# A message-passing layer on one core: three VectorE operations made in two halves each

## The chip, the cores and the metric

One Trainium2 chip, one of its cores. The metric is device microseconds of one execution of the whole program. In the profile PE is TensorE (matmul), PEld its weight load, DVE is VectorE, ACT is ScalarE, POOL is GpSimd and SP the engine that issues most DMAs; "L750" is line 750 of the kernel.

## The reference

One layer of a graph network with a residual: 6250 nodes of 128 features, 200000 edges sorted by `dst`, 20 edge features. With `ssp(x) = softplus(x) - log 2`:

```python
h = maximum(layernorm(x), 0)
xw = h @ W_in                                             # 6250 x 128
W_ij = (ssp(f_ij @ W_f1 + b_f1) @ W_f2 + b_f2) * cutoff   # 200000 x 128
x_ij = xw[dst] * W_ij                                     # idx_j = dst, gathered
out = segment_sum(x_ij, src, 6250)                        # idx_i = src, scattered
return x + ssp(out @ W_o1 + b_o1) @ W_o2 + b_o2
```

Everything is float32; the kernel gets there with sums of bfloat16 parts.

## The kernel before, in words

The edges are cut into chunks of 128; four chunks are a quad, so that 391 quads pass through one loop over `i`, a software pipeline in which iteration `i` works on different steps of several quads. The order inside an iteration is written out by hand: fixed steps and, between them, named points ("D0", "DM", "DR", "D2", "L" and so on) at which further steps are run. The table `AT` gives each step its offset in iterations and its point; the order on each engine is therefore the order of the program.

A quad's path: TensorE makes the filter's first layer `z` (L375), ScalarE its softplus by exponential and logarithm (L380, L385); TensorE gathers the rows of the nodes `xg` with a one-hot matrix (L563) and makes the second layer `W` (L571); ScalarE scales the gathered rows by the cutoff into `xc` (L576, four a quad); VectorE multiplies both (`s2_m`, L586). The message is then summed into the nodes in one of two ways, and the quads alternate between them.

- Scattered quads (184 by lists, 13 plain). The message tile is called `s` (or `m`). GpSimd adds its rows to one of four accumulators in DRAM by indirect DMAs (L648), 128 rows each, four per quad. A row index comes from a list: within a window of 16 such quads each lane finds which of its edges have the same node. The equality rows for it are made on VectorE by `l_eq` (L431, 92 times, one per two quads: four blocks of 128 x 2 columns, the nodes of a quad pair against each lane's own node), counted on TensorE and used for the index tile `lji`. Duplicates of a lane go through a list of their own in the accumulator, which is read back (`lm`, L517), summed by equal node on TensorE (`lsum`, L535), copied to `os` (L541) and scattered once more with the index `oji` (L838).
- Permuted quads (194). The message tile is called `pt`, four chunks of 388 columns: 128 for the message, 128 for its first remainder, 128 for its second and four more. A float32 message is split into three bfloat16 parts: a part is the upper half of the float32 word, and `part_rem` (L750, twice a quad, point "DM" and point "DR" of the same iteration) subtracts it from what is left. TensorE permutes the parts into groups of nodes with a one-hot matrix `pm` (VectorE, L736; TensorE, L762 and L785), ScalarE copies them to `sg` (L770), a DMA regroups them as `mst` (L777), and once in eight quads TensorE sums a round of them into units (`un`, L867) with one-hot matrices `so` (VectorE, L849), which VectorE adds to `accT` (L883).

The edge features are split into three bfloat16 parts in the same way, one block of 4096 edges at a time (49 blocks of 128 x 640 columns): `fb_1` and `fb_3` copy on ScalarE, `fb_2` makes the first remainder (L329), `fb_4` the second (L337), which a DMA writes to DRAM with the other two parts.

After the loop the accumulators are added, transposed and sent through the last two layers (lines from 1530 on).

```python
if first <= i - 1 < NQ:
    s2_m(i - 1)          # between the points "DM" and "DR"
```

Of the kernel before, what the change touches and what calls it, by code (L numbers as in the profile page):

```python
# [13 lines left out]
ALU = mybir.AluOpType  # L14
# [6 lines left out]
P = 128  # L21
# [55 lines left out]
def tile_gnn(ctx: ExitStack, tc: tile.TileContext, x, fB, cT, srcT, srcr, srci, dstr, win_, wf1, wf2, bias, bo1c, wo1,  # L77
             wo2, consts, ident, cmap, out, n_edges):
    nc = tc.nc
# [6 lines left out]
    FE = RB * BE // P  # L86
# [71 lines left out]
    fst = {}  # L158
# [8 lines left out]
    srcT_sb = cp.tile([P, EP // P], I16, name="srcT_sb")  # L167
# [166 lines left out]

    def fb_4(b):
        f3 = fst[b]["f3"]
        nc.vector.tensor_tensor(f3[:, 2], fst[b]["fr"], f3[:, 1], op=ALU.subtract)  # L337
        nc.sync.dma_start(fsd[b].rearrange("g (p e) -> p g e", p=P), f3)
        late["fb"] = fst.pop(b)["f"]

# [55 lines left out]
    sbs = {}  # L396
# [31 lines left out]
    def l_eq(k):  # L428
        n = 2 * k
        eq = wk.tile([P, 4, P, 2], BF16, tag="eql", name="eql", bufs=2)  # L430
        nc.vector.tensor_tensor(eq, sbs.pop(k).rearrange("p (b i t) -> p b i t", b=4, t=2),  # L431
                                srcT_sb[:, n * 4:n * 4 + 8].rearrange("p (b t) -> p b t", t=2).unsqueeze(2)
                                .to_broadcast([P, 4, P, 2]), op=ALU.is_equal)
        lst["eq", k] = eq

    def l_count(g):
# [303 lines left out]
    def high(t):  # L740
        return t.bitcast(BF16)[:, :, 1::2]
# [4 lines left out]

    def part_rem(q, k):
        pt = mp[q]["pt"]
        a = pt[:, :, (k - 1) * P:k * P]
        nc.vector.tensor_tensor(pt[:, :, k * P:(k + 1) * P], a, high(a), op=ALU.subtract)  # L750
        if k == 2:
            del st[q]

# [177 lines left out]
    with tc.manual_schedule():  # L931
# [72 lines left out]
        fb_3(0)  # L1004
        fb0 = fst[0]["f"]
        fb_4(0)
        rel0 = rel(0, 0, SC, "pt", pool=pg)
        prep_x1(0)
# [54 lines left out]
        def put(name, base, fn, *a, busy=()):  # L1063
            d, point = AT[name]
            i = max(clear(base + d, busy) if busy else base + d, 0)
            at(i, point, fn, *a)
            return i
# [51 lines left out]
        for b in range(1, NB):  # L1119
            t0 = 2  # L1120
            if b > 1:
                t0 = 8 * b - 8
                while t0 + 1 not in mpi or t0 + 1 in units:
                    t0 -= 1
                at(max(6, t0 - 6), "L", fb_load, b)
            if b > 1:
                at(max(8, t0 + AT["fmax"][0]), AT["fmax"][1], fb_max, b)
            else:
                at(7, "D2", fb_max, b)
            put("f1", t0, fb_1, b)  # L1130
            put("f2", t0, fb_2, b)
            put("f3", t0, fb_3, b)
            put("f4", t0, fb_4, b)
# [87 lines left out]
        if spread:  # L1221
            k = clear(mid + 9, busy, 2)
# [3 lines left out]
            k = clear(NQ - 1, busy, 2)  # L1226
# [19 lines left out]
        for g in range(len(tgroups)):  # L1246
            i = clear(max(r0_at + 1, ret_at + 12), units)
# [4 lines left out]
        for r in range(1 if min(2, NQ) and spread else 0, -(-len(mpq) // RKQ)):  # L1252
            i = mpq[RKQ * r]
            early = i < 8
            i = max(i, 4)
            put("rk_group", i, rank_group, r)
            put("rk_local", i, rank_local, r)
            k = put("rk_count", i, rank_count, r, busy=units)
            k = max(k + 1, i + AT["rk_own"][0])
            at(k, AT["rk_own"][1], rank_own, r)  # L1260
            k = clear(max(k, i + AT["rk_over"][0]), units)
            at(k, AT["rk_over"][1], rank_over, r)
            k = max(k + 1, i + AT["rk_slot"][0])
# [5 lines left out]
        for w in range(NW):  # L1269
            for g in range(wsize[w] // 4):  # L1270
                n = LB + SW * (w - 1) + 4 * g - LSHIFT
                i = splain[n] + 2 if w else 7 + 3 * g
                while w and (i not in mpi or i in units):
                    i -= 1
                for k in range(2):
                    kk = (LB + SW * w + 4 * g) // 2 + k
                    at(max(0, i + k - 2), "L", sb_load, kk)
                    put("l_eq", i + k, l_eq, kk)
                i = put("l_count", i, l_count, (LB + SW * w) // 4 + g, busy=units)
                k = put("l_dup", i, l_dup, w, g)  # L1280
            i = put("l_scan", i, l_scan, w)
            i = put("l_before", i - 1, l_before, w, busy=units)
# [3 lines left out]
            i = put("l_place", i, l_place, w, busy=units)  # L1286
            put("l_take", i, l_take, w)
            i = clear(max(wend[w] + wlag[w], uslots[-1][-1] + 1 if w == NW - 1 else 0), units)
# [4 lines left out]
            k = clear(i + AT["l_sum"][0], units)  # L1293
# [4 lines left out]
            k = put("l_int", k, over_int, ("L", w))  # L1298
# [4 lines left out]
        for q in mpq:  # L1303
            put("pm", q, perm_oh, q)
            put("rem1", q, part_rem, q, 1)
            put("rem2", q, part_rem, q, 2)
            put("ext", q, part_ext, q)
            if q + 4 in units:
# [12 lines left out]
            if mpi[q] % 2 or q == mpq[-1]:  # L1321
                k = mpq[mpi[q] + 1] if mpi[q] + 1 < len(mpq) else q + 3
# [4 lines left out]
                k = put("over_row", q, over_row, q, busy=units)  # L1327
                put("over_eq", k, over_eq, q)
                k = put("over_sum", q, over_sum, q, busy=units)
                put("over_copy", k, over_copy, q)  # L1330
                put("over_ji", k, over_ji, q)
                k = put("over_int", k, over_int, q)
# [122 lines left out]
    with tc.For_i(0, redo, 1):  # L1455
# [8 lines left out]
        with tc.For_i(0, trips, 1) as ci:  # L1464
# [15 lines left out]
            sb = wk.tile([P, P], I32, bufs=1, tag="oeq", name="fsb")  # L1480
# [27 lines left out]
            a = wk.tile([P, P], F32, tag="a", name="fa")  # L1508
# [7 lines left out]
            eq = wk.tile([P, P], F32, tag="eq", name="feq", bufs=3)  # L1516
# [15 lines left out]
    pt = ctx.enter_context(tc.tile_pool(name="pt", bufs=2, space=PSUM))  # L1532
# [150 lines left out]
def clear(i, busy, n=1):  # L1683
    while any(i + k in busy for k in range(n)):
        i += 1
    return i
# [114 lines left out]
```

## Time and profile before

| | |
|---|---|
| Three runs | 1875.44, 1885.99, 1892.93 us (median 1885.99) |
| The profiled execution | 1863.7 us |
| Its span, first to last instruction | 1861.9 us |
| TensorE matmul busy | 1663.2 us (89%) |
| VectorE busy | 1612.2 us (87%), 4740 instructions |
| ScalarE busy | 1466.1 us (79%) |
| GpSimd busy | 1486.0 us (80%), 949 instructions |
| Mean granted clock of TensorE | 0.971 of full speed |
| DMA | 339.68 MB, mean 182 GB/s |

Busy time counts overlapping instructions of an engine once. Instructions of one engine run in the order of the program. A row that names a line with "x4" groups four instructions that follow each other; "idle before" is the time in which the engine did nothing ahead of a group, and the arrow names what ended it. "issue" means that the profile shows nothing that the engine waited for. The shapes are partitions x elements. A timeline gives the start from the beginning of the span.

### The profile page before, as it was taken

How to read it: one execution, taken by the hardware profiler on the slowest of the kernel's cores; microseconds unless marked ns; L12 is line 12 of the kernel's file. 1: busy time of each engine (PE TensorE's matmuls, PEld its weight loads, DVE VectorE, ACT ScalarE, POOL GpSimd, SP SyncE). 2: the span in 40 equal slices, each digit the busy share in tenths (PEclk: the TensorE clock that was granted, in tenths of full speed). 3: DMA queues.
4: the chain of work that ended last, by engine and by line, in shares of the span. 5: the costliest groups of instructions: out<-in, count | busy, mean ns of one | idle time of the engine just before them, and what ended most of it. 6: DMA issues, size and time to landing. Idle time of an engine off the chain costs nothing.

```text
span 1861.9 us, 55503 instructions
## 1 busy us (share of the span) xinstructions
PE 1663.2 (89%) x19308; PEld 1114.3 (60%) x19308; DVE 1612.2 (87%) x4740; ACT 1466.1 (79%) x4068; POOL 1486.0 (80%) x949
## 2 busy tenths in 40 slices
PE   4779988999999989999898999999999999999846
PEld 3556656666666656656665666666666666666624
DVE  5778989899899989898899799899888899888746
ACT  4778878888888888888787888888888888888505
POOL 4567778888888888888888888888887888887875
PEclk9889999999999999999999999999999999999978
DMA  8998888888888888888887898888888888888847
GB/s 289 249 215 201 209 172 164 187 177 180 180 180 163 186 165 178 180 176 167 171 188 158 175 192 164 183 187 174 182 174 169 185 175 172 175 163 175 189 67 265
DMA packets 365471, 339.68 MB, mean 182 GB/s; under 512 B 86686, under 2 KB 328781, under 8 KB 365187
## 3 DMA queue, kind: packets, MB, share of 16 engines
q1 hardware_dynamic: 234005, 270.57, 49.7%
q0 software_dynamic: 130624, 65.33, 33.9%
q8 instruction: 152, 2.49, 0.5%
q14 instruction: 132, 1.08, 0.2%
q10 hardware_dynamic: 558, 0.20, 0.0%
HBM read 150.76 MB, written 108.08 MB: 139 GB/s over the span
## 4 chain that ended last, share of the span: by engine, by line
PE 36%; DVE 28%; DMA 12%; ACT 11%; issue 6%; SPq 4%; POOL 3%; DVEq 0%; ACTq 0%; POOLq 0%
PE un L867 10%; PE W L571 8%; PE pq L762 6%; DMA mst<-sg 5%; PE po L785 5%; DVE pt L750 4%; DVE accT L883 4%; ACT sg L770 4%; PE z L375 3%; DVE pm L736 3%; POOL acc L648 3%; ACT xc L576 3%; DVE s L586 2%; DMA acc<-s,lji 2%; DMA ft<-fsd 2%
## 5 line engine op out<-in xcount | busy, mean ns | idle before, releaser
L648 POOL DMA_INDIRECT acc<-s,lji x736 | 1182.1, 1606 | 244.1 <-issue 175.8
L576 ACT ACTIVATE xc<-xg,cb 128x128 f32<-128x128 f32 x1564 | 444.3, 370 | 7.1 <-PE xg L563 6.7
L571 PEld LDWEIGHTS W<-w,a 128*128 128x128 f32 x3128 | 426.5, 198 | 37.5 <-issue 23.7
L867 PE MATMUL un<-so,mst 32*128 32x392 bf16 x9312 | 431.6, 327 | 7.0 <-ACT sg L770 2.7
L571 PE MATMUL W<-w,a 128*128 128x128 f32 x3128 | 425.7, 280 | 0.1
L770 ACT CAST sg<-pq 128x388 bf16<-128x388 f32 x776 | 345.1, 493 | 78.5 <-DMA mst<-sg 38.1
L762 PE MATMUL pq<-pt,pm 128*128 128x388 bf16 x1552 | 328.3, 335 | 29.5 <-ACT mo L790 9.6
L867 PEld LDWEIGHTS <-mst 32*128 32x128 bf16 x9312 | 231.3, 93 | 155.5 <-issue 11.8
L385 ACT ACTIVATE a<-a,con 128x512 f32<-128x512 f32 x391 | 282.4, 722 | 11.6
L750 DVE TENSOR_TENSOR pt<-pt 128x512 f32<-128x512 f32 x388 | 263.6, 679 | 0.0
L380 ACT ACTIVATE a<-z 128x512 f32<-128x512 f32 x391 | 241.0, 616 | 25.7 <-PE z L375 25.5
L762 PEld LDWEIGHTS <-pm 128*128 128x128 bf16 x1552 | 146.3, 97 | 138.7 <-issue 46.0
L849 DVE TENSOR_SCALAR so<-iot,mst 128x392 bf16<-128x392 f16 x776 | 217.8, 330 | 5.3 <-PE un L867 4.7
L883 DVE TENSOR_TENSOR accT<-un,accT 128x392 f32<-128x392 f32 x368 | 182.0, 555 | 45.1 <-PE un L867 43.1
L736 DVE TENSOR_SCALAR pm<-iotp,pos 128x384 bf16<-128x384 f16 x776 | 208.9, 329 | 0.0
L648 POOL DMA_INDIRECT acc<-os,oji x109 | 175.0, 1606 | 37.4 <-issue 15.2
L375 PE MATMUL z<-ft,ws 123*128 123x512 bf16 x391 | 153.9, 394 | 41.9 <-ACT a L380 14.8
L586 DVE TENSOR_TENSOR s<-W,xc 128x512 f32<-128x512 f32 x184 | 125.7, 683 | 68.6 <-ACT xc L576 58.3
L586 DVE TENSOR_TENSOR pt<-W,xc 128x512 f32<-128x512 f32 x194 | 132.0, 680 | 47.7 <-ACT xc L576 27.1
L563 PE MATMUL xg<-wn,oh 63*128 63x128 bf16 x1564 | 156.5, 221 | 12.1 <-DVE oh L392 10.6
L785 PE MATMUL po<-pt,pm 128*128 128x387 bf16 x776 | 154.1, 341 | 0.9 <-DVE pt L750 0.7
L560 PE MATMUL W<-b2rep,onesb 64*128 64x512 bf16 x391 | 153.9, 393 | 0.0
(217 smaller groups left out, 1845.3 us busy)
## 6 DMA issues: line engine op xcount, KB each, us to landing
mst<-sg SPq DMA_DIRECT2D x776, 97.0 KB
sb<-src SPq DMA_DIRECT2D x98, 256.0 KB
rb<-reld SPq DMA_DIRECT2D x194, 128.0 KB
fsd<-f SPq DMA_DIRECT2D x49, 480.0 KB
ft<-fsd SPq DMA_DIRECT2D x96, 240.0 KB
fb<-in_fB_dram SPq DMA_DIRECT2D x49, 320.0 KB
ft<-fsd SPq DMA_DIRECT2D x96, 160.0 KB
acc<-s,lji POOLq DMA_INDIRECT x736
```

The lines of the kernel that those rows point to most:

```text
L385: nc.scalar.activation(a, a, AF.Ln, bias=half, scale=0.5)
L571: nc.tensor.matmul(W[:, c, :], st[q]["a"][:, c * P:(c + 1) * P], w2, start=False, stop=(c == 3))
L576: nc.scalar.mul(xc[:, c, :], st[q]["xg"][:, c, :], late["c", q // CQ][:, 4 * (q % CQ) + c:4 * (q % CQ) + c + 1])
L586: nc.vector.tensor_tensor(m[:, :, :P], st[q]["W"], st[q]["xc"], op=ALU.mult)
L648: nc.gpsimd.indirect_dma_start(out=accs[k][:rows, :], out_offset=bass.IndirectOffsetOnAxis(ap=ji, axis=0), in_=s, in_offset=None, compute_ ...
L736: nc.vector.tensor_scalar(pm[:, c], iotp, rk[r]["pos"][:, 4 * j + c:4 * j + c + 1], None, op0=ALU.is_equal)
L750: nc.vector.tensor_tensor(pt[:, :, k * P:(k + 1) * P], a, high(a), op=ALU.subtract)
L762: nc.tensor.matmul(t[:, :MW], mp[q]["pm"][:, c, s * P:(s + 1) * P], high(mp[q]["pt"][:, c:c + 1, :MW])[:, 0], start=(c == 2 * h), stop=(c ...
L770: nc.scalar.copy(mp[q]["sg", h][:, s], mp[q].pop(("q", k))[:, :MW])
L785: nc.tensor.matmul(t[:, :PW], mp[p]["pm"][:, c, GRP * BCAP:], high(mp[p]["pt"][:, c:c + 1, :PW])[:, 0], start=(p == qs[0] and c == 0), sto ...
L867: nc.tensor.matmul(ts[g][:, :GN], mp[q]["ms", s // 2][v, s % 2, k * P:(k + 1) * P], mp[q]["oh"][v], start=(q == qs[0] and k == 0), stop=(q ...
L883: nc.vector.tensor_tensor(v, t[:, :GN], v, op=ALU.add)
```

## The change

Each of three VectorE operations becomes two of half the width on the two halves of the same tiles: the remainders of a message (`part_rem`, chunks 0 and 1, then 2 and 3), the second remainder of the edge features (`fb_4`, columns 0 to 319, then 320 to 639) and the equality rows of the lists (`l_eq`, blocks 0 and 1, then 2 and 3).

```diff
     def fb_4(b):
         f3 = fst[b]["f3"]
-        nc.vector.tensor_tensor(f3[:, 2], fst[b]["fr"], f3[:, 1], op=ALU.subtract)
+        for h in range(2):
+            v = slice(h * FE // 2, (h + 1) * FE // 2)
+            nc.vector.tensor_tensor(f3[:, 2, v], fst[b]["fr"][:, v], f3[:, 1, v], op=ALU.subtract)
...
     def l_eq(k):
         n = 2 * k
         eq = wk.tile([P, 4, P, 2], BF16, tag="eql", name="eql", bufs=2)
-        nc.vector.tensor_tensor(eq, sbs.pop(k).rearrange("p (b i t) -> p b i t", b=4, t=2),
-                                srcT_sb[:, n * 4:n * 4 + 8].rearrange("p (b t) -> p b t", t=2).unsqueeze(2)
-                                .to_broadcast([P, 4, P, 2]), op=ALU.is_equal)
+        sb = sbs.pop(k).rearrange("p (b i t) -> p b i t", b=4, t=2)
+        ids = srcT_sb[:, n * 4:n * 4 + 8].rearrange("p (b t) -> p b t", t=2).unsqueeze(2)
+        for h in range(2):
+            b = slice(2 * h, 2 * h + 2)
+            nc.vector.tensor_tensor(eq[:, b], sb[:, b], ids[:, b].to_broadcast([P, 2, P, 2]), op=ALU.is_equal)
...
     def part_rem(q, k):
         pt = mp[q]["pt"]
-        a = pt[:, :, (k - 1) * P:k * P]
-        nc.vector.tensor_tensor(pt[:, :, k * P:(k + 1) * P], a, high(a), op=ALU.subtract)
+        for h in range(2):
+            a = pt[:, 2 * h:2 * h + 2, (k - 1) * P:k * P]
+            nc.vector.tensor_tensor(pt[:, 2 * h:2 * h + 2, k * P:(k + 1) * P], a, high(a), op=ALU.subtract)
```

The order on VectorE shows it at a place in the second half of the loop where all three stand close together. `pt` is the tile of a permuted quad, `s` that of a scattered one, `f` the feature parts, `eql` the equality rows. Before:

```order
L750 TENSOR_TENSOR pt<-pt 128x4x128
L586 TENSOR_TENSOR s<-W,xc 128x4x128
L750 TENSOR_TENSOR pt<-pt 128x4x128
L337 TENSOR_TENSOR f_25365<-fr,f_25365 128x640
L849 TENSOR_SCALAR so<-iot,mst 128x392 x3
L816 TENSOR_SCALAR oeq<-orow,ovs 128x128
L431 TENSOR_TENSOR eql<-sb,srcT_sb 128x1024
L834 SCALAR_TENSOR_TENSOR ojd<-os,con,ojd 128x1
```

And at the same place now, where lines behind the first edit carry other numbers (L755 for L750, L590 for L586, L339 for L337, L437 for L431):

```order
L755 TENSOR_TENSOR pt<-pt 128x2x128 x2
L590 TENSOR_TENSOR s<-W,xc 128x4x128
L755 TENSOR_TENSOR pt<-pt 128x2x128 x2
L339 TENSOR_TENSOR f_25725<-fr,f_25725 128x320 x2
L854 TENSOR_SCALAR so<-iot,mst 128x392 x3
L821 TENSOR_SCALAR oeq<-orow,ovs 128x128
L437 TENSOR_TENSOR eql<-sb,srcT_sb 128x512 x2
L839 SCALAR_TENSOR_TENSOR ojd<-os,con,ojd 128x1
```

Nothing changed places: the two halves stand where the whole stood. The order on the other engines is the same as before.

## Rows read from the trace of the kernel before

**Rows 1.** Span and granted clock of the core.

```profile
core 0: 1861.9 us, clock 0.971
```

**Rows 2.** Busy us, instructions of PE, PEld, DVE, ACT, POOL; then PEclk, DMA, GB/s.

```profile
300.00:1770.00 1470.00, 1374.78 (x16391) 915.00 (x16389) 1316.96 (x3908) 1218.36 (x3406) 1224.27 (x765) 0.99 0.85 176
```

**Rows 3.** POOL, 300:1770 us: busy us, mean ns | idle before, releasers.

```profile
L648 POOL DMA_INDIRECT acc<-s,lji x671 | 1077.7, 1606 | 213.8 <-issue 162.7 <-DMA acc<-s,lji 17.2 <-DVE accT L883 7.9
...
L648 POOL DMA_INDIRECT acc<-os,oji x94 | 149.2, 1587 | 32.3 <-issue 12.1 <-ACT sg L770 4.6 <-DMA acc<-s,lji 3.9
```

**Rows 4.** Waits of DVE, whole span: us in total, times, longest us.

```profile
DVE s L586 <- ACT xc L576: 58.3, 41, 4.4
...
DVE accT L883 <- PE un L867: 43.1, 45, 2.9
```

**Rows 5.** Chain that ended last, whole span: shares by line.

```profile
by line: PE un L867 9.5%; PE W L571 7.8%; issue 6.0%; PE pq L762 5.5%; DMA mst<-sg 4.9%; PE po L785 4.5%; DVE pt L750 3.7%; DVE accT L883 3.7%; ACT sg L770 3.6%; PE z L375 3.2%; DVE pm L736 3.0%; POOL acc L648 2.7%; ACT xc L576 2.7%; DVE s 
```

**Rows 6.** Timeline, tail: start us, us, engine, line [idle before <-releaser].

```profile
1792.68 0.49 PE L535 MATMUL lsum<-lm,leq 128*128 128x128 f32 x2 [1.72 <-DVE leq L529]
...
1794.94 1.54 POOL L648 DMA_INDIRECT acc<-s,lji  x1 [0.30 <-issue]
...
1800.34 1.84 PE L535 MATMUL lsum<-lm,leq 128*128 128x128 f32 x6 [7.17 <-DMA lm<-acc]
...
1802.99 0.29 ACT L838 ACTIVATE oji<-ojd,con 128x1 int32<-128x1 f32 x1 [0.29 <-DVE ojd L547]
...
1808.32 1.54 POOL L648 DMA_INDIRECT acc<-os,oji  x1 [0.30 <-DMA acc<-os,oji]
```

**Rows 7.** Groups by form, whole span: columns as in rows 3.

```profile
L750 DVE TENSOR_TENSOR pt<-pt 128x512 f32<-128x512 f32 x388 | 263.6, 679 | 0.0
...
L431 DVE TENSOR_TENSOR eql<-sb,srcT_sb 128x1024 bf16<-128x1024 int16 x92 | 62.3, 677 | 0.0
...
L337 DVE TENSOR_TENSOR f<-fr,f 128x640 bf16<-128x640 f32 x49 | 39.9, 814 | 0.9 <-ACT f L333 0.9
...
L648 POOL DMA_INDIRECT acc<-s,lji x736 | 1182.1, 1606 | 244.1 <-issue 175.8 <-DMA acc<-s,lji 25.5 <-DVE accT L883 7.9
...
L648 POOL DMA_INDIRECT acc<-os,oji x109 | 175.0, 1606 | 37.4 <-issue 15.2 <-ACT sg L770 4.6 <-DMA acc<-s,lji 3.9
...
L648 POOL DMA_INDIRECT acc<-s,ji x51 | 84.8, 1663 | 49.3 <-DMA acc<-s,ji 23.3 <-issue 6.7 <-DMA mst<-sg 6.6
```

**Rows 8.** Timeline of DVE from 1747 to 1751 us: columns as in rows 6.

```profile
1747.39 0.67 DVE L750 TENSOR_TENSOR pt<-pt 128x512 f32<-128x512 f32 x1
...
1747.98 0.67 DVE L586 TENSOR_TENSOR s<-W,xc 128x512 f32<-128x512 f32 x1
...
1750.11 0.74 DVE L417 TENSOR_TENSOR eq<-sb,srcT_sb 128x256 f32<-128x256 int16 x2
...
1750.78 0.20 DVE L834 SCALAR_TENSOR_TENSOR ojd<-os,con,ojd 128x1 f32<-128x1 f32 x1
```

**Rows 9.** Timeline of DVE and POOL, four pairs: columns as in rows 6.

```profile
303.91 0.68 DVE L750 TENSOR_TENSOR pt<-pt 128x512 f32<-128x512 f32 x1
...
304.26 1.75 POOL L648 DMA_INDIRECT acc<-s,lji  x1 [0.30 <-DVE s L586]
...
1728.87 0.68 DVE L750 TENSOR_TENSOR pt<-pt 128x512 f32<-128x512 f32 x1
...
1729.28 1.69 POOL L648 DMA_INDIRECT acc<-s,lji  x1 [0.31 <-issue]
...
328.79 0.68 DVE L431 TENSOR_TENSOR eql<-sb,srcT_sb 128x1024 bf16<-128x1024 int16 x1
...
328.86 2.02 POOL L648 DMA_INDIRECT acc<-s,lji  x1 [0.30 <-DVE oh L392]
...
905.96 1.29 DVE L736 TENSOR_SCALAR pm<-iotp,pos 128x384 bf16<-128x384 f16 x4
...
906.12 1.56 POOL L648 DMA_INDIRECT acc<-s,lji  x1 [0.74 <-DMA acc<-s,lji]
```

## The prediction

> **What bounds the kernel now.** I read the spans first, then the busy times of the middle stretch, then GpSimd's groups in it, the waits, the chain that ended last, and last the timeline of the tail. The profiled execution took 1863.7 us, of which 1861.9 are span [rows 1] and 1.8 lie around it; the median of the three runs shown is 1885.99, that is 22.3 more. I work the sum out on the profiled execution as a difference and add that to the median.
>
> From 300 to 1770 us four engines are all close to full [rows 2]: of 1470 us TensorE is busy 1374.8 (94%), VectorE 1317.0 (90%), ScalarE 1218.4 (83%). GpSimd shows only 1224.3 (83%), yet it is the fullest of all: its 765 scatters of that stretch are busy 1077.7 + 149.2 us and idle before them 213.8 + 32.3 us [rows 3], together 1473 us. Of that idle time 162.7 + 12.1 us have no releaser but "issue": it is the 0.30 us that stands before nearly every scatter in the timeline. So GpSimd sends a scatter every 1.54 + 0.30 us at best and from 300 us on hardly waits for anybody.
>
> There are then two streams. One is the scatters. The other is TensorE, ScalarE and VectorE handing work around: VectorE's longest waits are for ScalarE's scaled rows and TensorE's unit sums [rows 4], and in the chain no line has a tenth [rows 5]. Both must be done before the last scatter, and which comes last is seen in the tail. There the arithmetic needs only one list sum after 1792.68; GpSimd goes on with gaps of 0.30 us until the scatter at 1808.32 [rows 6]. So scatters end the edge phase now, and the arithmetic stream has some room.
>
> **The change part by part.** Nothing is removed or moved on any other engine; DMAs, queues and waits stay as they were. VectorE gets 388 + 92 + 49 = 529 more instructions [rows 7], because each of L750, L431 and L337 becomes two.
>
> *Price of one more instruction on VectorE.* Whole operation of 512 columns: starts at 1747.39, the next at 1747.98, so it holds the engine 0.59 to 0.60 us, less than its 679 ns, because the next one overlaps its end. Two operations of half the width on one tile are in the trace too: the pair of L417, 256 columns each, begins at 1750.11 and the next instruction at 1750.78: 0.67 us [rows 8]. A pair of halves thus costs 0.07 more than the whole. L337 gives the same: 814 ns at 640 columns against 679 at 512 is 1.05 ns a column, which leaves 679 - 538 = 141 ns of fixed time, of which some 80 overlap. L431 runs 1024 columns in 677 ns, a half-price column with the same fixed part, if the halves keep that rate. I take 0.067 us: 529 x 0.067 = 35.4 us of VectorE time. If nothing overlapped it would be 529 x 0.141 = 75 us; the overlapped pair is the nearer row. The second half of a remainder depends on a half written an operation or more earlier, so I price no new stall.
>
> [...]
>
> *How much of that reaches the end of the arithmetic stream.* L750 has 3.7% of the chain [rows 5], 69 us, which at 0.60 is 115 passes, 30% of its 388. With the same share for the others 0.30 x 529 = 158 halves lie on that chain: 158 x 0.067 = 10.6 us. The other 371 (24.8 us) lie in stretches where VectorE later waits, and the two waits shown alone are 58.3 + 43.1 us [rows 4]; they hide it. If that cover were gone the whole 35.4 would come. I take 11 us, range 8 to 35.
>
> *What the scatters gain.* A scatter takes 1.54 us when undisturbed and 1606, 1606 and 1663 ns on average [rows 7]: (66 x 736 + 66 x 109 + 123 x 51) ns = 62 us of excess. Where it comes from is seen by pairs in the timeline. A scatter that begins 0.35 us into an L750 takes 1.75, one that begins 0.41 us into it takes 1.69, one that begins 0.07 us into an L431 takes 2.02 [rows 9]. Each ends 0.55 to 0.56 us later, counted from the start of the VectorE operation, than its own 1.54 would: the scatter stands still until that operation is nearly over. From 300 us on 84 of 784 scatters begin inside an L750 (the first and the last are those two pairs) and lose 21.0 us, 18 inside an L431 (the first is shown) lose 4.0, 12 inside an L337 lose 1.0: 26 us. Four narrow operations in a row, L736, do not add up: a scatter that begins 0.16 us into such a run lost 0.02 [rows 9]. So GpSimd gets in between two operations, and a half holds it some 0.30 us instead of 0.56. Twice the chance to be hit at half the stay: the loss falls to 2 x 0.30^2 / 0.56^2 = 57%, a gain of 0.43 x 26 = 11 us. At the least it is nothing (if GpSimd does not get in between the halves), at the most 26.
>
> [...]
>
> *Where the two streams meet.* The last scatter began at 1808.32. It needs the list sum: two of its matmuls ran at 1792.68 to 1793.17, and from the next at 1800.34 to the end of the index at 1803.28 it took 2.94 us [rows 6]. With scatters in time that would be over at 1793.17 + 2.94 = 1796.1, and the scatter could begin at 1796.4: 11.9 us earlier. The list's last own scatter at 1794.94 lies 8.3 us ahead of that index and 13.4 ahead of the last scatter, so it does not decide. The edge phase thus moves by the later of two numbers: scatters -11 + 2 (the part of VectorE's delay before 300 us, 11 x 300 / 1770) = -9; arithmetic 11 - 11.9 = -0.9. The later one is -0.9. The final stage behind it is untouched. Sum: -0.9 us, so 1862.8 for the profiled execution and 1885.99 - 0.9 = 1885.1 for the median.
>
> **The rivals.** *A. VectorE becomes the bound (slower).* Mechanism: TensorE at 94% and VectorE at 90% wait on each other in turn, so that an addition beside the chain puts another path last. Place: the stretch 300 to 1770. Price: all 35.4 us arrive, 35.4 - 11.9 = 23.5 later: 1909.5. It decides from 12 us of delay on, and is over 1% from 11.9 + 18.9 = 31 us on. For it: 90 to 94% busy. Against it: over 100 us of waits on VectorE that can take it up.
>
> *B. The scatters decide alone (faster).* In runs without a profile the scatters may be further behind than here; then the room of the arithmetic is larger and the whole gain comes: 11 us, 1875; with all 26 us, 1860. For it: GpSimd has no free time from 300 us on [rows 3], and runs are 22.3 us longer than this execution without my seeing which stream makes them so. Against it: the tail shows 11.9 us of room and no more.
>
> *C. The split does nothing for GpSimd.* If the halves follow so closely that GpSimd does not get in, scatters stay and only the 2 us of early delay come: 1888. For it: the overlap of 80 ns between neighbours. Against it: the run of L736.
>
> [...]
>
> **How the numbers follow.** Forecast 0.48 (1876 to 1896 by its own bounds of -10 and +10), A 0.17, B 0.23, C 0.12. A measurement of this kernel tells about 1%, 18.9 us, from no change. Slower by more: four fifths of A, 0.13. Faster by more: in B the gain must be 19 of the 26 us at most, which I give half of B, 0.12. The rest, 0.75, is within 1%. The range 1867 to 1904 leaves out the far ends of A and B.
>
> **What would show it.** Right: 776, 184 and 98 instructions where L750, L431 and L337 had 388, 92 and 49, at some 410 ns for the first two; VectorE's busy time, overlaps counted once, up by some 35 us; scatter means falling from 1606 towards 1575; the last scatters with idle time before them above 0.30 us, waiting for the list sum. Wrong: scatter means that stay at 1606 (C), a tail with scatters still gapless and all earlier by 10 us or more (B), or unit sums that end 25 us later while GpSimd waits in the middle (A).

## The result, and the profile after

The changed kernel takes 1890.84 us (median of 22 runs, 1883.34 to 1899.56), the kernel before 1879.97 (22 runs, 1871.20 to 1892.93): ratio 1.0062, 95% interval 1.0046 to 1.0077, that is 10.9 us slower. The forecast was -0.9 us. The profiled execution of the changed kernel took 1895.27 us, 4.4 above its median; that of the kernel before took 1863.7, 7.5 below the lowest of the 22 runs. That second distance turns out to matter most below.

From the page of the changed kernel, its span and the busy times:

```profile
span 1893.5 us, 56032 instructions
...
PE 1686.3 (89%) x19308; PEld 1129.4 (60%) x19308; DVE 1646.7 (87%) x5269; ACT 1472.0 (78%) x4068; POOL 1492.9 (79%) x949
```

VectorE has its 529 instructions more and is busy 34.5 us longer than before; the sum had 35.4. The groups by form, columns as in [rows 3], answer to [rows 7]:

```profile
L652 POOL DMA_INDIRECT acc<-s,lji x736 | 1188.9, 1615 | 253.5 <-issue 174.1 <-DMA acc<-s,lji 27.9 <-DVE pt L755 9.8
L755 DVE TENSOR_TENSOR pt<-pt 128x256 f32<-128x256 f32 x776 | 291.4, 416 | 0.0
L652 POOL DMA_INDIRECT acc<-os,oji x109 | 175.8, 1613 | 55.4 <-issue 15.5 <-DVE xl L1224 9.3 <-ACT pt L761 7.0
L652 POOL DMA_INDIRECT acc<-s,ji x51 | 84.3, 1653 | 48.1 <-DMA acc<-s,ji 24.0 <-issue 13.5 <-ACT sg L775 3.0
L437 DVE TENSOR_TENSOR eql<-sb,srcT_sb 128x512 bf16<-128x512 int16 x184 | 69.2, 416 | 0.2 <-DMA sb<-src 0.2
L339 DVE TENSOR_TENSOR f<-fr,f 128x320 bf16<-128x320 f32 x98 | 43.4, 483 | 0.9 <-ACT f L333 0.9
```

Halves take 416, 416 and 483 ns, and the scatters' means are 1615, 1613 and 1653 ns where [rows 7] has 1606, 1606 and 1663: their expected fall towards 1575 did not come. The tail, in the timeline of the changed kernel (columns as in [rows 6]), is the opposite of [rows 6]:

```profile
1827.40 1.54 POOL L652 DMA_INDIRECT acc<-os,oji  x1 [0.30 <-DMA acc<-s,ji]
...
1829.24 1.54 POOL L652 DMA_INDIRECT acc<-os,oji  x1 [0.30 <-issue]
...
1836.42 0.35 DVE L533 TENSOR_SCALAR leq<-orow,idl 128x128 f32<-128x128 f32 x1
...
1839.54 0.30 ACT L843 ACTIVATE oji<-ojd,con 128x1 int32<-128x1 f32 x1 [0.29 <-DVE ojd L551]
...
1840.11 2.01 POOL L652 DMA_INDIRECT acc<-os,oji  x1 [9.33 <-DVE xl L1224]
```

The reader is to see the 9.33 us ahead of the last scatter. GpSimd had nothing left to do at 1830.78; `leq`, the last VectorE operation of the lists, ends only at 1836.77, the index `oji` at 1839.84, and 0.27 us later the scatter starts (the releaser that the row names, `xl`, is another operation of those moments). Here the arithmetic ends the edge phase, 9 us behind the scatters. The chain that ended last says the same: shares by line, where [rows 5] had 9.5% for the unit sums and 2.7% for the scatters,

```profile
by line: PE un L872 13.4%; PE W L575 9.4%; PE pq L767 7.1%; issue 6.4%; PE z L377 4.4%; PE po L790 4.3%; DVE pt L755 4.0%; DVE accT L888 3.8%; DVE pm L740 2.9%; ACT sg L775 2.8%; DMA mst<-sg 2.3%; ACT xc L580 1.9%; DVE so L854 1.9%; DVE s L
```

with no scatter among the lines shown. Something else is new in this trace, in the waits of three engines (us in total, times, longest us), of VectorE, ScalarE and TensorE:

```profile
DVE s L590 <- issue: 33.9, 27, 4.1
...
ACT ojd L805 <- issue: 19.2, 20, 2.4
...
PE pq L767 <- issue: 8.6, 14, 2.2
```

These are gaps of up to 4 us in which an engine waits for nothing that the profile shows. In the profile of the kernel before, VectorE's messages (`s`) wait 6.7 us in that way in 5 places, the index `ojd` on ScalarE 0.4 us, and `pq` has no such row. The first of these rows in the kernel before:

```profile
DVE s L586 <- issue: 6.7, 5, 2.5
```

I call them gaps. They are no cost of the halves: e6 below has them without any halves. What the halves cost differs with them.

### The profile page after: what moved, and what is told of

The parts are those of the page before. It is cut to its first block, busy times and chain, and to the rows that moved or that the text cites. A ratio compares the mean times of both kernels' runs of the same rounds, so it can differ in the third digit from the quotient of the medians.

```text
span 1893.5 us, 56032 instructions
## 1 busy us (share of the span) xinstructions
PE 1686.3 (89%) x19308; PEld 1129.4 (60%) x19308; DVE 1646.7 (87%) x5269; ACT 1472.0 (78%) x4068; POOL 1492.9 (79%) x949
## 4 chain that ended last, share of the span: by engine, by line
PE 47%; DVE 26%; ACT 8%; DMA 7%; issue 6%; SPq 5%; POOL 1%; DVEq 0%; ACTq 0%; POOLq 0%
PE un L872 13%; PE W L575 9%; PE pq L767 7%; PE z L377 4%; PE po L790 4%; DVE pt L755 4%; DVE accT L888 4%; DVE pm L740 3%; ACT sg L775 3%; DMA mst<-sg 2%; ACT xc L580 2%; DVE so L854 2%; DVE s L590 2%; DVE pt L590 2%; PE xg L567 2%
## 5 line engine op out<-in xcount | busy, mean ns | idle before, releaser
L652 POOL DMA_INDIRECT acc<-s,lji x736 | 1188.9, 1615 | 253.5 <-issue 174.1
L767 PE MATMUL pq<-pt,pm 128*128 128x388 bf16 x1552 | 332.6, 337 | 39.0 <-ACT mo L795 9.0
L872 PEld LDWEIGHTS <-mst 32*128 32x128 bf16 x9312 | 235.7, 93 | 158.4 <-issue 19.0
L755 DVE TENSOR_TENSOR pt<-pt 128x256 f32<-128x256 f32 x776 | 291.4, 416 | 0.0
L854 DVE TENSOR_SCALAR so<-iot,mst 128x392 bf16<-128x392 f16 x776 | 222.6, 337 | 4.5 <-PE un L872 3.5
L652 POOL DMA_INDIRECT acc<-os,oji x109 | 175.8, 1613 | 55.4 <-issue 15.5
L740 DVE TENSOR_SCALAR pm<-iotp,pos 128x384 bf16<-128x384 f16 x776 | 203.1, 322 | 0.0
L590 DVE TENSOR_TENSOR s<-W,xc 128x512 f32<-128x512 f32 x184 | 125.9, 684 | 64.2 <-issue 33.9
L590 DVE TENSOR_TENSOR pt<-W,xc 128x512 f32<-128x512 f32 x194 | 132.5, 683 | 40.9 <-ACT xc L580 28.2
L567 PE MATMUL xg<-wn,oh 63*128 63x128 bf16 x1564 | 156.8, 221 | 11.9 <-DVE oh L394 5.1
```

Source lines behind the costliest of these rows:

```text
L590: nc.vector.tensor_tensor(m[:, :, :P], st[q]["W"], st[q]["xc"], op=ALU.mult)
L652: nc.gpsimd.indirect_dma_start(out=accs[k][:rows, :], out_offset=bass.IndirectOffsetOnAxis(ap=ji, axis=0), in_=s, in_offset=None, compute_ ...
L740: nc.vector.tensor_scalar(pm[:, c], iotp, rk[r]["pos"][:, 4 * j + c:4 * j + c + 1], None, op0=ALU.is_equal)
L755: nc.vector.tensor_tensor(pt[:, 2 * h:2 * h + 2, k * P:(k + 1) * P], a, high(a), op=ALU.subtract)
L767: nc.tensor.matmul(t[:, :MW], mp[q]["pm"][:, c, s * P:(s + 1) * P], high(mp[q]["pt"][:, c:c + 1, :MW])[:, 0], start=(c == 2 * h), stop=(c ...
L854: nc.vector.tensor_scalar(so, iotw[:, :GN], w[:, 3 * P // 2:3 * P // 2 + 1], None, op0=ALU.is_equal)
```

## The experiments

Eighteen kernels ran in five groups; those of one group ran on one chip and share their runs of the kernel before, and the five chips or occasions differ:

| group | runs | kernel before, median us | gaps in the traces |
|---|---|---|---|
| first | e1 to e4 | 1864.63 | no |
| second | e5 to e7 | 1880.63 | yes |
| third | e8 to e11 | 1868.79 | no |
| fourth | e12 to e15 | 1880.14 | yes |
| fifth | e16 to e18 | 1868.36 | no |

The profile before (1863.7 us, 6.7 us of gaps ahead of the messages) belongs with the groups without gaps, the profile after with those that have them. The timed runs of the result have no trace; by the median of the kernel before (1879.97 us) they belong with the groups that have gaps. The second and third group ran on a chip of the same number, so the gaps are not a property of one chip. "Arithmetic end" below is the end of the last `leq` in the run's timeline.

### First group: the kernel before again, the two parts, and small instructions

e1 is the kernel before, unchanged.

> The kernel before, unchanged, for a second profile: 0 us. Theory T1 (the arithmetic stream of TensorE, ScalarE and VectorE ends last in an ordinary execution; the 11.9 us of room that I read in the tail belonged to one unusually short execution, 1863.7 us): an execution near the median of 1880 us shows a last scatter with more than 3 us of idle time before it. Theory T2 (the scatters end last, and halves behind each other hold GpSimd longer): the tail is again gapless, 0.30 us between scatters.

Measured: 1870.18 us against 1864.63, ratio 1.0029 (1.0010 to 1.0049). Two copies of one program differ by 0.29%, so I read nothing from a single difference below some 0.3%. Its tail in the timeline:

```profile
1796.10 0.34 DVE L529 TENSOR_SCALAR leq<-orow,idl 128x128 f32<-128x128 f32 x1
...
1813.20 1.54 POOL L648 DMA_INDIRECT acc<-os,oji  x1 [0.30 <-issue]
...
1815.05 1.54 POOL L648 DMA_INDIRECT acc<-os,oji  x1 [0.30 <-DMA acc<-os,oji]
```

As in [rows 6], the scatters end without a pause, and the last one starts 18.95 us after the start of the last `leq`; in the tail of the changed kernel, where it waits for that operation, it is 3.69 us. The difference, 15.3 us, is the room here. T1 spoke of an execution near 1880 us, which this one, of 1870.18 us, is not: there is room at 1870 us too, and T1 is left for e6.

e2 halves the remainders alone (the third edit of the diff shown above):

```diff
-        a = pt[:, :, (k - 1) * P:k * P]
-        nc.vector.tensor_tensor(pt[:, :, k * P:(k + 1) * P], a, high(a), op=ALU.subtract)
+        for h in range(2):
+            a = pt[:, 2 * h:2 * h + 2, (k - 1) * P:k * P]
+            nc.vector.tensor_tensor(pt[:, 2 * h:2 * h + 2, k * P:(k + 1) * P], a, high(a), op=ALU.subtract)
```

> Only the message remainders are halved: 388 more VectorE instructions, 388 x 0.067 = 26 us of VectorE time. T1: the share that arrived in the whole change, 10.9 of 34.5 us (0.31), of 26 us: +8 us, and the last scatter waits for the list sum. T2: the remainders make 98 of the 134 starts inside the three operations, so +8 us as well, but with gapless scatters in the tail and a longer mean of a scatter. The prediction on record: -5 to +1 us.

Measured: 1860.85, ratio 0.9985 (0.9965 to 1.0004). The mean of a list scatter is 1608 ns in its trace, so T2's longer holds are not there. e3 has the other two edits alone (`l_eq` and `fb_4`, as in the diff shown above).

> Only the equality rows and the second feature remainders are halved: 141 more VectorE instructions, 9.4 us. T1: 0.31 x 9.4 = +3 us. T2: the 36 of 134 starts, +3 us, with a longer mean of a scatter. A third reading, that the lists' path is what counts because the last scatter waits for a list: +8 to +11 us.

Measured: 1870.36, ratio 1.0021 (1.0001 to 1.0041). e4 leaves all operations whole and sets one small one behind each:

```diff
+    tiny = cp.tile([P, 1], F32, name="tiny")
...
         nc.vector.tensor_tensor(f3[:, 2], fst[b]["fr"], f3[:, 1], op=ALU.subtract)
+        nc.vector.memset(tiny, 0.0)
```

(and the same line behind the operations of `l_eq` and `part_rem`).

> No operation is halved; behind each of the 529 whole ones stands a VectorE memset of 128 x 1, which adds the time of an instruction and leaves all widths. T1: it costs 0.31 of the VectorE time that it adds, +11 us at 0.067 us each, up to +25 us at 0.15 us each. T2: widths and so the holds of GpSimd are as before: 0 to +2 us.

Measured: 1864.46, ratio 0.9990 (0.9974 to 1.0006). It is a weaker dose than I had thought: in its timeline a whole remainder and its memset hold VectorE 608 ns where the remainder alone holds it 601 (medians from the start of one to the start of the next operation), 7 ns instead of 69. It shows only that, without gaps, 529 more instructions cost nothing by their number.

So none of the pieces costs anything here that can be told from the difference of two copies. Either the result needed both parts, or the occasion.

### Second group: the whole change, and a larger dose

> The whole change once more. The first profile of it has gaps without a releaser ('issue') on VectorE (33.9 us ahead of the message products alone), ScalarE and TensorE, and register moves of SyncE of several hundred ns where 29 to 38 are usual; no profile of the kernel before or of its parts has them. Theory P (these gaps belong to this program, 529 instructions longer): +10 to +12 us again, with the gaps in the new profile. Theory E (they belonged to the chip and the execution): the parts add up, -0.15% + 0.21%, so between -3 and +5 us, SyncE's moves are back at 29 to 38 ns, the arithmetic stream ends near 1797 us as in the parts, and the scatters end last again.

Measured for e5: 1897.74 against 1880.63, ratio 1.0093 (1.0058 to 1.0128), +17.1 us (+10.9 to +24.1), with gaps: theory P had +10 to +12. e6 is the kernel before beside it.

> The kernel before, unchanged, as the measure of what two copies of one program differ by: within 0.3% (it was +0.29% on its first copy). Theory P: no gaps of 'issue' on VectorE beyond 10 us. Theory E: if the chip is one of the slower kind (kernel before near 1880 us), the gaps show here too.

Measured: 1878.19, ratio 0.9995 (0.9968 to 1.0021). Its trace has the gaps as well, so theory P falls. The waits of VectorE, ScalarE and TensorE in e6, the kernel before:

```profile
DVE s L586 <- issue: 24.7, 20, 3.8
...
ACT ojd L800 <- issue: 22.4, 23, 2.8
...
PE pq L762 <- issue: 6.2, 13, 0.6
```

and the same in e1, the same program:

```profile
DVE s L586 <- issue: 3.0, 4, 1.0
...
ACT ojd L800 <- issue: 2.7, 3, 1.5
...
PE z L375 <- issue: 0.3, 1, 0.3
```

Added up over 300 to 1770 us, VectorE has 29.8 us of gaps in e6 and 6.1 in e1, ScalarE 44.1 and 4.0, TensorE 26.0 and 0.3. SyncE's register moves at L368, 29 or 38 ns in e1, last up to 695 ns in e6 (29 to 38 ns in the profile before; up to 697 in the profile after, where 71 of 586 last over 100 ns). The tail that goes with it, in the timeline of e6 (an execution of 1873.23 us, the shortest of its twelve):

```profile
1814.15 0.34 DVE L529 TENSOR_SCALAR leq<-orow,idl 128x128 f32<-128x128 f32 x1
...
1815.95 1.54 POOL L648 DMA_INDIRECT acc<-os,oji  x1 [0.30 <-issue]
...
1818.00 2.01 POOL L648 DMA_INDIRECT acc<-os,oji  x1 [0.51 <-DVE xl L1219]
```

The arithmetic ends at 1814.49, 18 us later than in e1, and the last scatter starts 3 us later, 0.51 us after the one before it, 0.21 more than the usual 0.30: both streams end together, and the room of the arithmetic is gone before anything is changed. T1 is borne out in that, though it had named 3 us of idle time and not 0.51. That the gaps themselves delay the arithmetic, and not something else that comes with them, is not shown: of the chain that ended last "issue" has 5.6% in e6 and 6.3% in e1 (whole span). In e5, with the halves, the last scatter has 16.75 us of idle time before it.

e7 makes the remainders in four pieces:

```diff
-        a = pt[:, :, (k - 1) * P:k * P]
-        nc.vector.tensor_tensor(pt[:, :, k * P:(k + 1) * P], a, high(a), op=ALU.subtract)
+        for h in range(4):
+            a = pt[:, h:h + 1, (k - 1) * P:k * P]
+            nc.vector.tensor_tensor(pt[:, h:h + 1, k * P:(k + 1) * P], a, high(a), op=ALU.subtract)
```

> The message remainders in four pieces, 1164 more instructions, 1164 x 0.067 = 78 us of VectorE time (three times that of the halves alone). Arithmetic bound (0.31 of it): +24 us. Room of some 12 us ahead of the scatters: 0.31 x 78 - 12 = +12 us, with idle time before the last scatter. No effect of VectorE's additions on the end at all: 0 to +3 us, scatters gapless in the tail.

Measured: 1911.32, ratio 1.0167 (1.0129 to 1.0205), +30.7 us. Four pieces hold VectorE 807 ns, so the dose is 388 x (807 - 601) = 80 us, and 0.38 of it arrives. With the gaps there is next to no room to subtract (0.21 us in e6).

### Third group: the whole change without gaps, and light scatters

> The whole change a third time, on whichever of the two chips so far it falls. Theory R (the room is the chip's: where SyncE's register moves take hundreds of ns and engines have gaps of 'issue', the kernel before at 1880 us already ends with the arithmetic stream, room 2 us; where these are missing, the kernel before at 1865 us ends with the scatters, room 12 us): on the first kind +11 to +17 us with idle time before the last scatter, on the second 0 to +3 us with gapless scatters. Theory P (the program itself): +11 to +17 us on both.

Measured for e8: 1872.21 against 1868.79, ratio 1.0020 (1.0005 to 1.0035), +3.4 us, and no gaps. The same program costs +10.9 and +17.1 with them. Its tail in the timeline:

```profile
1812.77 0.35 DVE L533 TENSOR_SCALAR leq<-orow,idl 128x128 f32<-128x128 f32 x1
...
1820.68 1.54 POOL L652 DMA_INDIRECT acc<-os,oji  x1 [0.30 <-issue]
...
1822.53 1.54 POOL L652 DMA_INDIRECT acc<-os,oji  x1 [0.30 <-issue]
```

The scatters end last, without a pause, as theory R says for executions without gaps; that the condition is the chip's, as R had it, is wrong, since the second group ran on a chip of the same number with gaps. This execution (1878.75) is the longest of its twelve, so I take no difference from its ends. e9 and e10 are the two parts again.

> Only the remainders halved, 26 us of VectorE time. On the second kind -0.15% again. On the first kind: theory R with a share of 0.45 (the arithmetic of the remainders in four pieces ended 34.9 us later for 78 us): +12 us at the arithmetic's end, +10 us in the time. A rival there (the feature write, which now waits on SyncE by an instruction of its own for the second half and holds the loads behind it, makes the rest): 0 to +4 us.

> Only the equality rows and the second feature remainders halved, 9.4 us of VectorE time. On the second kind +0.2% again. On the first kind: theory R +4 us at the arithmetic's end, 0 to +2 us in the time; the rival with the feature write on SyncE: +8 to +11 us.

Measured: e9 1867.43, ratio 0.9999 (0.9983 to 1.0014); e10 1870.49, ratio 1.0010 (0.9990 to 1.0030). As in the first group.

e11 takes the scatters off the end by giving each 64 rows instead of 128; half of the messages' rows are left out.

```diff
-        nc.gpsimd.indirect_dma_start(out=accs[k][:rows, :], out_offset=bass.IndirectOffsetOnAxis(ap=ji, axis=0), in_=s,
+        nc.gpsimd.indirect_dma_start(out=accs[k][:rows, :], out_offset=bass.IndirectOffsetOnAxis(ap=ji[:64], axis=0), in_=s[:64],
```

> The kernel before with scatters of 64 rows in place of 128 (half of the rows of the messages are left out), so that GpSimd is done early and only the arithmetic sets the end. Theory R on the first kind: no more than -2 to -5 us, the arithmetic ends near 1814 us as before. On the second kind: -10 to -14 us, the room. If the arithmetic is itself held back by the scatters (by buffers that come free late), it is more: -20 us or below on either kind.

Measured: 1825.64, 43.2 us less than the kernel before. The last scatter now waits 19.85 us, and the arithmetic ends at 1764.9, 28 to 32 us earlier than in the two profiles of the kernel before without gaps (1792.62 and 1796.45). That is the third case of the expectation: the two streams are not independent, as I had them; lighter scatters let the arithmetic go faster. Which link does it (the DMA engines are busy 0.71 of the middle stretch instead of 0.84 in e1; VectorE's messages `s` wait 22.3 us for the scatters' DMAs in e1, 1.1 in the profile before and not at all in e11) these runs do not separate.

### Fourth group: with gaps

> The changed kernel with scatters of 64 rows (half of the messages' rows are left out), so that the scatters do not set the end. Against the kernel before with the same scatters it is the price of the halves for the arithmetic stream alone. Theory V (VectorE's time arrives in the arithmetic stream whenever nothing else is later): 0.3 to 0.64 of 35.4 us, +11 to +22 us, in the time itself. Theory G (the halves cost through GpSimd, whose scatters they hold): 0 to +3 us.

> The kernel before with scatters of 64 rows again, the base for the run above: -40 to -45 us without the gaps of 'issue'; -25 to -35 us with them, because they delay the arithmetic stream by some 17 us.

Measured: e12 (the changed kernel with light scatters) 1940.17, e13 (the kernel before with light scatters) 1928.09: a difference of 12.1 us with the scatters off the end, 0.34 of 35.4. That is theory V's size, but the six runs of e12 lie 30 us apart (1921.49 to 1951.08), and by resampling the difference of the medians may be anything from -2 to +22 us. This pair does not decide between V and G; e17 below does. The second expectation missed by far: light scatters made the kernel 48 us slower than the kernel before (1880.14) instead of 25 to 35 faster. From 300 to 1770 us, e11 and then e13 (columns as in [rows 2]):

```profile
300.00:1770.00 1470.00, 1385.30 (x16721) 924.51 (x16719) 1310.94 (x3945) 1213.63 (x3396) 1184.44 (x776) 0.99 0.71 159
```

```profile
300.00:1770.00 1470.00, 1347.24 (x15683) 892.02 (x15672) 1251.75 (x3749) 1179.35 (x3280) 1135.11 (x735) 0.97 0.69 151
```

The same program issues 16721 matmuls in this stretch without gaps and 15683 with them. Gaps of TensorE add up to 56.3 us in e13 and 0.4 in e11 in this stretch, and the granted clock is 0.97 instead of 0.99, an estimate of 0.02 x 1470 = 29 us. If both add in full, that is most of the 102 us between the two medians; the sum was not tested, and why gaps hit this version harder than e6 (26.0 us) stays open.

> The message remainders in four pieces, 78 us of VectorE time. With the gaps of 'issue' it was +30.7 us. Without them, theory V with a room of 12 us ahead of the scatters: 0.45 x 78 - 12 = +23 us, idle time before the last scatter. If the additions of VectorE are hidden without the gaps: 0 to +5 us, as with two pieces.

> Equality rows and second feature remainders halved, alone. Without the gaps +0.1 to +0.2% again. With them: theory V +4 us at the arithmetic's end and in the time; the rival with the feature write on SyncE +8 to +11 us.

Measured: e14 1909.46, ratio 1.0173 (1.0142 to 1.0203), +29.3 us, as e7. e15 1882.90, ratio 1.0025 (1.0001 to 1.0048), +2.8 us; its arithmetic ends at 1820.8 against 1814.5 in e6. That is theory V's size; the interval, +0.2 to +9.0 us, just reaches the 8 to 11 us of a second cause on SyncE and makes it unlikely.

### Fifth group: the dose without gaps

> Four pieces again, for the dose without the gaps of 'issue', should this run have none. Without them, theory V with a room of 12 us: +23 us and idle time before the last scatter; if VectorE's additions are hidden there: 0 to +5 us. With the gaps: +29 to +31 us as twice before.

Measured for e16: 1881.98 against 1868.36, ratio 1.0069 (1.0053 to 1.0085), +13.6 us where it was +30.7 and +29.3 with gaps. The timeline shows the room used up:

```profile
1823.57 0.34 DVE L529 TENSOR_SCALAR leq<-orow,idl 128x128 f32<-128x128 f32 x1
...
1823.82 1.54 POOL L648 DMA_INDIRECT acc<-os,oji  x1 [0.30 <-DMA acc<-s,ji]
...
1827.26 2.01 POOL L648 DMA_INDIRECT acc<-os,oji  x1 [1.90 <-DVE xl L1220]
```

The arithmetic ends at 1823.91, 27.5 us later than in e1, which is 0.34 of 80; 27.5 - 13.6 = 14 us of it were hidden (18 against the profile before, whose arithmetic ends at 1792.62). The +23 us of the expectation came from too large a share, 0.45.

> The changed kernel with scatters of 64 rows (half of the messages' rows left out). Without the gaps the kernel before with such scatters took 43 us less than the kernel before; theory V puts the halves' 0.3 to 0.64 of 35.4 us on top: 11 to 22 us of the 43 are lost, so -32 to -21 us against the kernel before. If VectorE's additions are hidden without the gaps: -43 to -38 us. With the gaps: +60 us as measured.

Measured: 1838.42, 29.9 us below the kernel before, where e11 without the halves was 43.2 below: 13.2 us of price, 0.37 of 35.4, in the time itself once the scatters are out of the way. e11 and e17 are of two groups, but the kernel before took 1868.79 and 1868.36 us there, and every run of e17 (1834.27 us and up) lies above every run of e11 (up to 1828.02). So theory V stands, and theory G falls, without gaps. The last scatter of e17 waits 18.37 us.

> Remainders alone, 26 us of VectorE time. With the gaps, theory V: the whole change less what the other part cost there (10.9 to 17.1 less 2.8 us), +8 to +14 us, by its dose (0.45 x 26) +12 us. Without them: 0 us as twice before.

Measured: 1862.91, ratio 0.9964 (0.9946 to 0.9982), again without gaps, a little below the 0 us expected. Over three groups the remainders alone stand at 0.9985, 0.9999 and 0.9964, on average 3.5 us faster; two copies of one program differ by as much (e1). The remainders alone with gaps were not measured. The scatters of e18, by form:

```profile
L648 POOL DMA_INDIRECT acc<-s,lji x736 | 1174.7, 1596 | 247.4 <-issue 177.6 <-DMA acc<-s,lji 31.0 <-DVE accT L884 8.2
L648 POOL DMA_INDIRECT acc<-os,oji x109 | 174.9, 1605 | 34.9 <-issue 15.2 <-ACT sg L771 4.6 <-DMA acc<-s,lji 4.2
L648 POOL DMA_INDIRECT acc<-s,ji x51 | 85.2, 1670 | 54.8 <-DMA acc<-s,ji 17.0 <-DMA acc<-zero 9.4 <-issue 8.2
```

## Why the prediction was wrong

**The price of one more VectorE instruction: right.** A pair of halves holds VectorE 670 ns, a whole remainder 601 (medians of some 335 each): 69 ns against the 67 of the sum. No run shows the 0.15 us an instruction that the expectation of e4 allowed for at the most: back to back a second half costs these 69 ns, and e4's memset 7.

**How much reaches the end of the arithmetic stream: right, a little low.** The sum had 11 us. Where the scatters are off the end it is 13.2 us without gaps (and 12.1 with them, from runs that vary too much to be a test); the larger dose gives 0.34 to 0.38 of its 80 us, where the chain's share had given 0.30. The profiles after with gaps end their arithmetic some 22 us later than e6; part of that is which execution was profiled, since e6's lies 5.0 us below its median and that of the changed kernel 4.4 above.

**What the scatters gain: none of it reached the time.** The step said that GpSimd gets in between two halves and that 11 us come of it. Two pairs of the timeline of the changed kernel, VectorE and GpSimd, show why it is half true:

```profile
1275.12 0.75 DVE L755 TENSOR_TENSOR pt<-pt 128x256 f32<-128x256 f32 x2
1275.24 1.71 POOL L652 DMA_INDIRECT acc<-s,lji  x1 [0.30 <-issue]
...
1319.81 0.75 DVE L755 TENSOR_TENSOR pt<-pt 128x256 f32<-128x256 f32 x2
1319.94 2.04 POOL L652 DMA_INDIRECT acc<-s,lji  x1 [0.30 <-issue]
```

Both scatters begin 0.12 to 0.13 us into the first half. The first loses 0.17 us: it is let go at the end of that half. The second loses 0.50 us: it is held through the second half too. In the changed kernel's profile 83 scatters begin in a first half; 56 of them go on by 0.40 us after its start, 21 only at the end of the second half, and six are held beyond it, like the one that begins at 1063.56 and takes 2.87 us, through the features' halves that follow. So a scatter can be held through several instructions in a row. Why 56 of them go on after the first half and 27 do not, the trace does not show.

The sum over scatters, [rows 7] and its like, is 1441.9 and 1452.6 us in the two profiles of the kernel before without gaps and 1452.5 in the one with them; 1439.6, 1445.0 and 1434.8 with the remainders halved (no gaps); 1455.6, 1451.1 (no gaps) and 1456.8 (gaps) with the other two; with all, 1437.0 without gaps and 1449.0 and 1448.5 with them. Two profiles of one program differ by 10.7 us, as much as the forecast gain of 11, so the size of the gain is not settled: compared within one condition, all halves stand 5 to 16 us lower without gaps and 4 lower with them. In the time nothing of it arrives. By the step the scatters should have ended 9 us earlier; in e8, where they do end last, the time is 3.4 us longer (+0.9 to +6.5). Its scatters, by form, show what stands against the gain:

```profile
L652 POOL DMA_INDIRECT acc<-s,lji x736 | 1181.9, 1606 | 248.5 <-issue 175.3 <-DMA acc<-s,lji 23.0 <-DVE accT L888 13.2
L652 POOL DMA_INDIRECT acc<-os,oji x109 | 174.1, 1598 | 53.7 <-ACT pt L761 13.2 <-issue 12.9 <-DMA acc<-s,lji 6.8
L652 POOL DMA_INDIRECT acc<-s,ji x51 | 81.0, 1589 | 49.9 <-DMA acc<-s,ji 27.7 <-issue 7.3 <-DMA acc<-zero 4.7
```

Idle time before them is 248.5 + 53.7 + 49.9 = 352.1 us, where [rows 7] has 330.8: 21 us more waiting than before, against 5 to 16 us less time at work. The step let the scatters' end follow their own duration alone and left out what they wait for. This is one profile, of an execution 6.5 us above its median, so it points to the mechanism and does not give its size. In number rival C's +2 us was nearer than the forecast; its mechanism, that GpSimd does not get in between the halves, holds for 27 of the 83.

**Where the two streams meet: this step failed.** It took the 11.9 us of room from [rows 6] and added the difference to the median of the timed runs, as if the same stream ended last in both. But the profiled execution is one without gaps (room of 11.9 us there, 15.3 in e1, 14 to 18 by e16), and the timed runs are, by their time, those with gaps, in which the arithmetic ends as late as the scatters already: 0.21 us of room in e6. With no room the prediction's own term for the arithmetic, 11 us, is the result, 10.9; that it fits so closely is in part luck, since the same change took +17.1 in e5. Without gaps the sum comes near in the number, -0.9 against +3.4 us, but not in the mechanism: the scatters still end last, and not 9 us earlier. The 22.3 us between the profiled execution and the median stood in the working and were carried along as an offset. As far as e6 tells, they were the arithmetic's: there it ends 22 us later than in the profile before, the last scatter 10 us later. The text met them under rival B, and gave them to the scatters: for the larger part, the wrong stream.

**The rivals.** A named VectorE's additions as the bound, with all 35.4 us arriving; 0.31 to 0.48 of them arrive with gaps. B is ruled out: with gaps the scatters do not decide, and without them the time rose. What would show the forecast right (idle time before the last scatter) was seen in the profile after, 9.33 us of it, but as the mark of a loss: the prediction would have had it come from earlier scatters, and it came from later arithmetic.

## What to carry to other kernels

When the profiled execution lies outside the range of the timed runs, find out first which stream makes up the difference: room read from its tail is room of that execution, and a term that it hides may arrive whole in the others. Here a split cost 69 ns of a busy engine, about 0.36 of that reached the end of its stream, and it came into the time at once where no other stream ended later. Do not count on another engine to get in between two pieces that are issued back to back (here 56 of 83 scatters did), nor on its stream to end earlier when it does: read what else that stream waits for.

## What was not expected of the hardware

One program has two conditions here that no source line sets: with and without gaps of "issue" on VectorE, ScalarE and TensorE (29.8, 44.1 and 26.0 us against 6.1, 4.0 and 0.3 from 300 to 1770 us) and long register moves on SyncE. In the groups without gaps the kernel before takes 1865 to 1869 us, in those with gaps 1880; the kernel with light scatters takes 1825.64 and 1928.09. All profiled runs of a group shared the condition, in groups on a chip of the same number it differed, and the traces do not name its cause. That gaps are waits for instructions to be loaded was a guess of mine, and the packets of the instruction queues do not bear it out: in e6 33 of the 156 gaps overlap one, 21%, and in the profile after 33 of 148, 22%, as many as times taken at random there give (22%); the packets of queue 8 have the same median in e6 as in e1, 1.01 us (0.98 in the profile before, 0.99 in the profile after). And lighter scatters let the arithmetic end 28 to 32 us earlier without gaps: the streams that I had set side by side are coupled.
